# A table of ranks, and fewer planning passes, for the order of a four-stage transformer kernel

## The chip, the cores and the metric

The kernel runs on one core of a Trainium2 chip. A core has five engines that run at the same time, each with its own queue of instructions taken in order: TensorE (PE: matmuls, and PEld for its weight loads), VectorE (DVE), ScalarE (ACT), GpSimd (POOL) and SyncE (SP, which here only issues DMAs). The metric is the device time of one execution in microseconds (us); less is better.

## What is computed

The input x has 16 sequences of 256 tokens with 128 features, float32. It goes through six residual steps, of four kinds:

```python
x = x + 0.5 * _L0_ffn_ref(_layernorm(x), ...)   # experts: 8, two per token, and one shared
x = x + _L0_attn_ref(_layernorm(x), ...)        # differential attention, 16 heads, causal
x = x + 0.5 * _L0_ffn_ref(_layernorm(x), ...)   # the same experts again
x = x + 0.5 * _L1_ffn_ref(_layernorm(x), ...)   # a quantised MLP, 128-512-128
x = x + _L1_attn_ref(_layernorm(x), ...)        # linear attention, a scan over tokens
x = x + 0.5 * _L1_ffn_ref(_layernorm(x), ...)   # the quantised MLP again
```

Nothing in the change touches what is computed. What differs is in which order each engine does it.

## The kernel before

**Tiling.** The tokens are cut into 8 blocks of 512 (two sequences each), and a block stays on chip as `xs[k]` from its load to its store. The two expert steps are called "a" and "b". Each treats the blocks in groups: for "a" 0, 1, 2-3, 4-5, 6-7, for "b" 0-1, 2-3, 4-5, 6, 7. Group a0 computes all eight experts densely. All other groups route: GpSimd scatters normalised rows by indirect DMAs into slots in DRAM sorted by expert (`scatter`, L714), tiles of 128 slots are loaded and multiplied by their expert's weights (`rows`, `expert`), and GpSimd gathers the results back, adding them to `xs[k]` (`gather`, L966, eight indirect DMAs for each block and two for each 128 rows). Attention runs per sequence b: `project` and `rope` make the keys and queries, `maxima` (L1247, L1264) finds row maxima on VectorE, `weights` (L1302, L1323) takes exponentials on ScalarE, `values` and `output` finish. The scores of a step fill four banks of PSUM at once, and there is one such tile, "s". The quantised MLPs are `qa` and `qb`, the linear attention is `l` with eight steps `l k f` per block (load, product, scan L1701, product L1705, matmul).

**Order.** The program is written as some hundreds of tasks, which are Python generators. A task yields one operation at a time with the engines that can do it and a planned duration. The class `Order` keeps a planned time for each engine and each buffer, and picks what is issued next: on the engine that can start first, among the operations that can start within 0.05 us of the first, the one of lowest rank.

```python
            pick = min((c for c in cands if c[0] <= first + self.SLACK), key=lambda c: (c[1], c[0]))
```

The order picked is the order of the instructions in each engine's queue. On the chip an engine then follows its queue strictly: an instruction that waits for a semaphore holds back everything behind it. Where an operation can go to two engines (a copy to ScalarE or VectorE, a product to VectorE or GpSimd), the planned times choose.

**Ranks.** A task's rank comes from the program: 1 to 5 for the groups of "a", 4.5 and 9 down to 6 for those of "b" and the quantised and linear steps behind them, 0.5 and 0.6 for `project` and `output`, 1.5 to 2.8 for loads and the clearing of slots. The attention steps `maxima`, `weights` and `values` carry ranks of their own, between -1.0 and about -0.8, on each operation or on the task. Tasks of positive rank are shifted by kind, which is the task's name up to its first dot; there are 360 such kinds:

```python
        if rank > 0.0:

            kind = name.split(".")[0]
            self.seen.add(kind)
            rank += self.moved.get(kind, 0.0)
```

A TensorE operation of rank below 0.0 counts as urgent: when one becomes ready soon, an operation of higher rank that would delay it is put off (L213 to L222).

**Search.** `best_order` (L306) runs the whole program dry, on objects that do nothing, to get the planned end of a set of shifts. It begins with no shifts. In each further pass it gives 5 kinds new random shifts between -3 and 3, and keeps them if the planned end falls. After 60 passes the program runs once more, with the best shifts, and issues real instructions. All this happens on the host before the launch.

**The planner's durations** are formulas and constants in the operations. Those that the text below speaks of:

```python
    return k * (0.16 + n * 0.00104)                              # e_dve
    return k * (0.25 + n * 0.0029)                               # e_pool
                g = yield Op([("POOL", 1.6)], kb=1, need=need)   # one gather
        g = yield dve(1.4)                                       # the scan of linear_f
                t = end + 2.0                                    # landing of a POOL DMA
```

Other names: `attention loads` and `attention loads 2` load the attention's weights (the second ends in the product hnw, L1014, on VectorE); `stats` (L505) is bn_stats and bn_aggr, L512 and L513; `gated` (L728) makes the gated product hr of an expert, with the tanh form (L740, L749, L754 or L760) until the attention's last exponential is issued, and the Silu form (L733, L737) otherwise.

Of the kernel before, what the change touches and what calls it, by code (L numbers as in the profile page):

```python
# [270 lines left out]

PLANS, MOVES, SPREAD = 60, 5, 3.0

# [20 lines left out]
@with_exitstack  # L298
def block_kernel(ctx: ExitStack, tc: tile.TileContext, t_in: dict, out: bass.AP):
    ctx.enter_context(tc.manual_schedule())  # L300
    pools = [ctx.enter_context(tc.tile_pool(name=name, bufs=1)) for name in ("const", "small", "work")]
    pools.append(ctx.enter_context(tc.tile_pool(name="ps", bufs=1, space=PSUM)))
    program(best_order(), tc.nc, tc, *pools, t_in, out)


def best_order():  # L306


    rng = random.Random(3)
    best, moved = math.inf, {}  # L310
    for _ in range(PLANS):
        trial = dict(moved)
        if best < math.inf:
            for name in rng.sample(sorted(names), MOVES):
                trial[name] = rng.uniform(-SPREAD, SPREAD)
        order = Order(trial)
        dry = Dry()
        try:
            program(order, dry, dry, dry, dry, dry, dry, dry, dry)
        except AssertionError:  # L320
            continue
        if order.end < best:
            best, moved = order.end, trial
            names = order.seen
    return Order(moved)
# [1526 lines left out]
```

## Time and profile before

| | |
|---|---|
| median of 3 runs | 1313.22 us (1311.86 to 1316.47) |
| profiled execution | 1316.87 us |
| its span, first to last instruction | 1315.2 us |
| mean granted TensorE clock | 0.965 |
| DVE waits longest in all for | ACT thr L740, 40.8 us in 38 times |
| POOL waits longest in all for | DVE mv L513, 116.4 us in 25 times |
| PE waits longest in all for | POOL state L1705, 13.9 us in 6 times |
| 120 gathers on POOL | 194.1 us busy |
| last attention exponential | before 1000 us of the span |

A profile is of one execution. "Busy" is the time in which an engine had an instruction in hand; TensorE's ends are modelled, so a busy PE isn't PE at its peak. The granted clock is the share of full speed that TensorE was allowed. A wait names the instruction that released it last. A line such as `L409 PE MATMUL` is that of a helper, so groups are told apart by the tiles: `pgu` and `poy` are an expert's first and second product, `hr` the gated product between them, `scores` the attention scores, `qpad` their maxima, `ex` their exponentials, `pol` and `state` the linear attention, `phq`, `poq` and `yq` the quantised MLP.

### The profile page before, as it was taken

What the parts mean: (1) busy time and instruction counts of PE and PEld (TensorE: products, weight loads), DVE (VectorE), ACT (ScalarE), POOL (GpSimd) and SP (SyncE); (2) the same over time, 40 slices, a digit from 0 to 9 for tenths busy, and PEclk for the clock granted to TensorE, in tenths of its full rate; (3) what the DMA queues carried; (4) which work ended last, traced back from release to release, by engine and by line L of the source; (5) the groups of instructions that cost most, each with busy time, mean ns of one, the idle gap of its engine ahead of it and who ended that gap; (6) DMA issues with size and microseconds to landing.
All of it is one profiled execution on the core that took longest, in us unless ns stands there. A gap on an engine that the chain in (4) does not pass through costs nothing. (4 is left out here: it accounts for less than half of the span.)

```text
span 1315.2 us, 32976 instructions
## 1 busy us (share of the span) xinstructions
PE 1175.2 (89%) x12480; PEld 853.7 (65%) x12480; DVE 897.6 (68%) x2059; ACT 655.5 (50%) x1163; POOL 821.7 (62%) x972
## 2 busy tenths in 40 slices
PE   6797889999899979998987799999999869898888
PEld 3465666676576667766754577767567657675566
DVE  5465667776678655594776568768748757587993
ACT  2153456554555544645633475664564524544424
POOL 4213546738862882384458735477867788779874
PEclk9898999999999989998998799999999989998989
DMA  4675563525344335445222333314445766642331
GB/s 127 147 194 132 140 161 87 143 67 125 88 128 128 52 86 159 127 105 125 69 82 27 88 90 104 88 52 110 100 129 161 206 158 169 169 127 77 93 100 33
DMA packets 213006, 149.68 MB, mean 114 GB/s; under 512 B 18544, under 2 KB 200944, under 8 KB 212848
## 3 DMA queue, kind: packets, MB, share of 16 engines
q1 hardware_dynamic: 155376, 113.70, 31.0%
q0 software_dynamic: 21120, 15.81, 6.8%
q10 hardware_dynamic: 36352, 18.07, 4.8%
q8 instruction: 99, 1.62, 0.5%
q14 instruction: 59, 0.48, 0.1%
HBM read 117.32 MB, written 30.19 MB: 112 GB/s over the span
## 5 line engine op out<-in xcount | busy, mean ns | idle before, releaser
L409 PE MATMUL pgu<-xTg,wst 128*128 128x128 f32 x1464 | 218.5, 285 | 10.9 <-DMA wst<-in_w_dram 6.1
L409 PEld LDWEIGHTS pgu<-xTg,wst 128*128 128x128 f32 x1464 | 188.7, 195 | 37.8 <-issue 19.2
L1264 DVE TENSOR_REDUCE qpad<-scores 128x8 f32<-128x2048 f32 x64 | 146.4, 2288 | 40.2 <-PE scores L413 39.7
L1323 ACT ACTIVATE ex<-scores 128x2048 f32<-128x2048 f32 x64 | 120.2, 1878 | 85.6 <-PE scores L413 85.5
L409 PE MATMUL poy<-wst,hr 128*128 128x128 f32 x732 | 117.3, 287 | 20.2 <-POOL hr L754 9.1
L413 PE MATMUL scores<-qm,kT 32*128 32x256 f32 (+1 forms) x2048 | 114.1, 349 | 16.1 <-DVE qpad L1264 9.8
L413 PE MATMUL scores<-kT,qT 32*128 32x512 f32 (+1 forms) x1024 | 113.4, 536 | 14.0 <-ACT ex L1323 4.9
L409 PEld LDWEIGHTS poy<-wst,hr 128*128 128x128 f32 x732 | 98.5, 196 | 36.8 <-DVE hr L737 11.7
L966 POOL DMA_INDIRECT x<-slots_yb,pos x64 | 106.5, 1664 | 17.5 <-issue 15.8
L928 ACT ACTIVATE y<-poy,xg 128x128 f32<-128x128 f32 x162 | 59.2, 368 | 98.0 <-PE poy L409 93.1
L413 PEld LDWEIGHTS scores<-qm,kT 32*128 32x128 f32 x2048 | 79.6, 189 | 41.5 <-DVE qpad L1264 16.2
L413 PE MATMUL pav<-ex,vaug 128*32 128x512 f32 (+1 forms) x1024 | 98.4, 503 | 2.3 <-ACT ex L1323 2.2
L966 POOL DMA_INDIRECT x<-slots_ya,pos x56 | 87.6, 1565 | 17.2 <-issue 14.2
L500 POOL TENSOR_TENSOR rr<-ss,mhalf 128x32 f32<-128x32 f32 x16 | 87.9, 5492 | 16.5 <-DVE ss L1401 16.4
L714 POOL DMA_INDIRECT slots_xa<-xng,pos x56 | 56.0, 1001 | 61.3 <-DMA slots_xa<-xng,pos 30.4
L413 PEld LDWEIGHTS pol<-owr,state 128*128 128x128 f32 x512 | 68.5, 207 | 37.9 <-POOL state L1705 18.9
L413 PE MATMUL pol<-owr,state 128*128 128x128 f32 x512 | 74.8, 295 | 20.3 <-POOL state L1705 13.9
L516 POOL TENSOR_SCALAR rs<-mv 128x4 f32<-128x4 f32 (+1 forms) x56 | 19.8, 353 | 117.2 <-DVE mv L513 116.4
L1701 DVE TENSOR_TENSOR_SCAN state<-lam,kv 128x512 f32<-128x512 f32 x64 | 90.3, 1423 | 1.4 <-POOL kv L1698 1.1
L413 PEld LDWEIGHTS <-shift 32*128 32x128 bf16 x3072 | 59.2, 95 | 48.3 <-issue 37.5
L714 POOL DMA_INDIRECT slots_xb<-xng,pos x64 | 67.6, 1057 | 35.4 <-DMA slots_xb<-xng,pos 13.5
L1247 DVE TENSOR_REDUCE qpad<-scores 128x16 f32<-128x2048 f32 x32 | 73.2, 2289 | 22.7 <-PE scores L413 22.4
(250 smaller groups left out, 2651.8 us busy)
## 6 DMA issues: line engine op xcount, KB each, us to landing
wst<-in_w_dram SPq DMA_DIRECT2D x573, 128.0 KB
kv<-values_l SPq DMA_DIRECT2D x64, 256.0 KB
xg<-slots_xb SPq DMA_DIRECT2D x21, 258.0 KB
slots_yb<-y ACTq DMA_DIRECT2D x21, 256.0 KB
xg<-slots_xa SPq DMA_DIRECT2D x18, 258.0 KB
slots_ya<-y ACTq DMA_DIRECT2D x18, 256.0 KB
slots_xa<-zero ACTq DMA_DIRECT2D x10, 258.0 KB
slots_xb<-zero ACTq DMA_DIRECT2D x10, 258.0 KB
```

Of the source, the lines that this page charges most:

```text
L409: nc.tensor.matmul(dst, lhsT, rhs, start=start, stop=stop)
L413: nc.tensor.matmul(dst, lhsT, rhs, start=start, stop=stop, skip_group_check=True)
L500: nc.gpsimd.tensor_tensor(dst, src, mhalf[:, :n], ALU.pow)
L516: nc.gpsimd.tensor_scalar(rs, mv[:, 0:nt, 1], LN_EPS, None, ALU.add)
L714: ins = nc.gpsimd.indirect_dma_start(sx, by_rows(r["pos"][:, i * nt + t : i * nt + t + 1]), xn[:, t, :], None,)
L928: nc.scalar.activation(y[:, i, :], po[:, 0:D], AF.Copy, scale=xg[:, i, D:SW])
L966: nc.gpsimd.indirect_dma_start(x[:, t, :], None, sy, by_rows(r["pos"][:, a : a + 1]), compute_op=ALU.add,)
L1247: nc.vector.tensor_reduce(qp[:, 0, T0 : T0 + 2, :, :, HD].rearrange("p t m g -> p m t g"), s.rearrange("p m (t g n) -> p m t g n", t=2, g= ...
L1264: nc.vector.tensor_reduce(qp[:, 1, T, :, :, HD], s.rearrange("p m (g n) -> p m g n", g=G), AX.X, ALU.max, negate=True)
L1323: nc.scalar.activation(ex0, s, AF.Exp, scale=1.0 / math.sqrt(HD))
L1701: nc.vector.tensor_tensor_scan(state, lam, kv, 0.0, ALU.mult, ALU.add)
```

## The change

The search no longer begins with no shifts but with a table of them, `MOVED`, that stands in the source. It has shifts for 228 of the 360 kinds, each with one decimal, between -3.0 and 2.9. The first pass plans with the table as it is; the other 19 change 5 kinds each, as before, with the same seed. The planner, the durations and the program are otherwise the same.

```diff
-PLANS, MOVES, SPREAD = 60, 5, 3.0
+MOVED = {
+    "attention consts": 2.6, "attention loads": 2.0, "attention loads 2": -1.0, "attention pads": 0.8,
...
+    "experts a2": 2.1, "experts a3": -0.1, "experts a4": 0.1, "experts b1": -0.8, "experts b2": -2.5,
+    "gather a1": -1.0, "gather a2": -1.0, "gather a3": 2.2, "gather a4": 1.7, "gather b0": 1.6,
+    "gather b4": 0.6, "l 0": 0.4, "l 0 0": 0.2, "l 0 1": -0.8, "l 0 2": 1.3, "l 0 3": 0.7, "l 0 4": 0.5,
...
+    "output 1": 1.2, "output 11": 2.5, "output 14": -0.1, "output 2": 1.6, "output 3": 1.9, "output 5": 2.9,
+    "output 6": 0.5, "output 8": -2.3, "output 9": 0.2, "project 0": -2.5, "project 10": -1.8,
+    "project 11": -1.9, "project 14": 2.2, "project 15": -1.9, "project 2": -0.4, "project 5": -0.8,
+    "project 7": -0.9, "project 9": -1.3, "qa 0 0": -0.6, "qa 0 1": 2.7, "qa 0 2": -2.0, "qa 1": -1.0,
...
+    "route b4": 1.8, "rows a4": 0.6, "scatter a1": 1.3, "scatter a2": 2.3, "scatter a3": -0.0,
+    "scatter a4": 2.7, "scatter b0": -1.7, "scatter b1": -1.3, "scatter b2": -0.3, "scatter b3": -0.4,
...
+    "softmax b4": 1.8, "x1": -1.3, "x2": 0.7, "x5": 0.9, "x6": -1.7, "x7": 1.0,
+}
+
+
+PLANS, MOVES, SPREAD = 20, 5, 3.0
...
     rng = random.Random(3)
-    best, moved = math.inf, {}
+    best, moved = math.inf, dict(MOVED)
     for _ in range(PLANS):
         trial = dict(moved)
         if best < math.inf:
```

## The prediction

> **What bounds the kernel now.** I read the busy shares first, then the slices, three stages, and in each stage the largest holes of TensorE with what ended them.
>
> ```profile
> PE 1175.2 (89%) x12480; PEld 853.7 (65%) x12480; DVE 897.6 (68%) x2059; ACT 655.5 (50%) x1163; POOL 821.7 (62%) x972
> PE   6797889999899979998987799999999869898888
> POOL 4213546738862882384458735477867788779874
> PEclk9898999999999989998998799999999989998989
> ```
>
> TensorE is the bound: 1175.2 of 1315.2 us. After the start the PE digit falls to 7 or 6 in slices 15, 22, 23 and 33; POOL stands at 7 or 8 in each, and the granted clock falls to 8 or 7. The stages:
>
> ```profile
> 0.00:150.00 150.00, 118.05 (x755) 82.40 (x755) 85.21 (x322) 52.24 (x100) 49.71 (x125) 0.94 0.61 152
> 150.00:990.00 840.00, 774.82 (x9984) 552.86 (x9977) 570.28 (x1257) 458.21 (x761) 520.02 (x601) 0.97 0.39 101
> 990.00:1315.20 325.20, 282.32 (x1756) 218.43 (x1748) 242.12 (x480) 145.04 (x304) 251.98 (x247) 0.95 0.47 129
> ```
>
> The second column is the stretch, then busy PE, PEld, DVE, ACT and POOL, then clock, DMA share, GB/s. PE idles 32.0 us in the dense start, 65.2 under attention, 42.9 in the tail: 140.0 us, the most that any reordering could win at unchanged PE work. The largest hole under attention:
>
> ```profile
> 717.88 2.09 PE L413 MATMUL scores<-kT,qT 32*128 32x512 f32 x8
> ...
> 722.98 2.09 PE L413 MATMUL scores<-kT,qT 32*128 32x256 f32 x16
> ...
> 727.89 2.09 PE L413 MATMUL scores<-qm,kT 32*128 32x256 f32 x16 [2.39 <-DVE qpad L1247]
> ...
> 732.22 2.09 PE L413 MATMUL scores<-kT,qT 32*128 32x512 f32 x8 [2.03 <-ACT ex L1323]
> ```
>
> Only attention is left to issue there: one scores tile, filled, reduced, filled again. The filler (experts, quantised layers, linear attention) hangs on sixteen gathers:
>
> ```profile
> 722.57 1.55 POOL L966 DMA_INDIRECT x<-slots_yb,pos  x1 [0.30 <-issue]
> 724.42 1.56 POOL L966 DMA_INDIRECT x<-slots_yb,pos  x1 [0.30 <-issue]
> 726.28 1.55 POOL L966 DMA_INDIRECT x<-slots_yb,pos  x1 [0.30 <-issue]
> ```
>
> The tail's largest hole is of another kind:
>
> ```profile
> 1053.63 0.29 DVE L512 BATCH_NORM_STATS2 st<-x 128x6 f32<-128x128 f32 x1 [4.62 <-DMA x<-slots_yb,pos]
> ...
> 1055.18 0.39 DVE L737 SCALAR_TENSOR_TENSOR hr<-thr,pgu 128x256 f32<-128x256 f32 x1
> ```
> ```profile
> 1055.62 1.23 PE L409 MATMUL poy<-wst,hr 128*128 128x128 f32 x4 [6.06 <-DVE hr L737]
> ```
>
> VectorE's queue held a statistics instruction whose gathered rows had not landed; the expert's product stood behind it, and PE waited 6.06 us for that product.
>
> **Nothing is added on the device but order.** The planner runs before launch, so the table and the drop from 60 passes to 20 cost no device time. Each task still issues its operations and DMAs; which engine takes an elementwise operation, and which form the gated product has, follow the new plan. PE work therefore stays at 1175 us, moved by its clock alone. The kernel before ends its search with 29 of 360 kinds moved. The table moves 228 and leaves 132; if each accepted pass places 5 of 360 at random, (1 - 5/360)^n = 132/360 gives n = 72 accepted passes, against 6 before. It is a much longer climb on the planner's own clock, so what counts is how far that clock agrees with the chip.
>
> **Where the planner is right, it can gain.** It knows coarse things: that attention without filler starves PE, that a block's work waits for its gathers. Three holes have the size for it.
> - 706 to 740 us: the seven gaps of PE are 1.05+1.49+2.82+1.98+2.39+2.03+0.71 = 12.5 us. The matmuls between run slowly too: a scores block takes 2.09 us where the same block took 1.14 at 713.14 us (four blocks, 3.8 us), the value product 2.79 against 1.50 (1.3), the masks 0.4 more. That is 12.5 + 5.5 = 18.0 us. The Trainium skill, "TensorE: Matmul & The Clock Gate" (Part 1), ties the half clock to an idle window of about 3.4 us; by the rule no gap here (longest 2.82) would cost more than itself, so 12.5. The trace has clock 0.50 at 720 to 730 us with PE busy 5.63 of 10, so I take the row: 18.0.
> - 1048 to 1100 us: PE is busy 36.79 of 52 at clock 0.87: 15.2 idle and 36.79 x 0.13 = 4.8 slow, 20.0 us.
> - 50 to 70 us: VectorE waits 11.59 us for the load of the head norm (L1014), with the product of the shared expert behind it; PE idles 9.0 us and is busy 10.99 at 0.74, 2.9 slow: 11.9 us. "attention loads" goes up 2.0 and "attention loads 2" down 1.0, so the load and this instruction both move. It may vanish or come back elsewhere: no sign can be read.
>
> Together 49.9 us. The ranks reach them: gathers of a3, a4 and b0 and the scatters and experts around them get shifts of 1 to 3, and project 0, 10, 11 and 15 fall below -1.0, ahead of all attention steps. What ranks can't reach are the attention steps (each operation carries its own rank), the first 12.4 us without PE (the first loads are not moved) and the arithmetic. SP's queue changes order with them, and that costs nothing: its weight loads wait 436.5 us in all for buffers that the expert products free, and PE waits only 6.1 us for weights; without that cover each late load would cost PE up to the 2.5 us that is the longest now. A gap filled here takes filler from elsewhere, and there is no row for a hole that stays closed: the bounds are 0 and 49.9, and I take half, 25, because two of the three are of kinds that the planner sees.
>
> **Where the planner is wrong, the order costs.** A gather is planned at 1.6 us of POOL, and the trace starts one every 1.86 us (722.57, 724.42, 726.28). Sixteen in a row end 16 x 0.26 = 4.2 us later than planned. What is queued next on POOL, or on VectorE behind a wait for the landing, is late by that much, and PE stands on it:
>
> ```profile
> PE poy L409 <- POOL hr L754: 9.1, 3, 4.2
> PE poy L409 <- DVE hr L737: 8.0, 3, 6.1
> ```
>
> Three bursts do this now: 4.23 us at 464, 4.2 at 590, 6.06 at 1050: 14.5 us, 4.8 each, of nine bursts (120 gathers, 7.5 of 16). A climb removes idle time which the planner sees and knows nothing of this slack. I take five bursts in place of three: 2 x 4.8 = 9.7 us back. Bounds: none stalls (-14.5) to all nine (+29).
>
> The same goes for VectorE beside POOL. The Trainium skill, "SBUF — State Buffer" (SBUF: two separate sides), says that a VectorE operation with two SBUF inputs and a GpSimd one that reads SBUF take a shared port pair in turn, the later one blocked for the whole of the other; the planner lets them overlap. Row: the 64 scans (L1701) take 1216 ns in the median, 1423 in the mean, so 64 x 0.207 = 13.2 us are lost now. If every scan met a POOL product (median 1316 ns) from its start, the rule would give 64 x 1.316 = 84 us. POOL and VectorE are both over 74% busy in the tail already and mostly don't collide; by the row a new order moves the 13.2 us by a few either way, and I take 0.
>
> **Sum.** -25 + 9.7 = -15 us. The profiled execution took 1316.87 us, 1.7 around its span of 1315.2; it should read about 1301. The median of the runs shown is 1313.22, 3.7 below the profiled execution; from it the forecast is 1313.2 - 15 = 1298 us.
>
> **Rivals.**
> - *The plan is tighter than the chip (slower).* Place: POOL's queue after each gather burst, and VectorE's queue behind statistics that wait for landings. Price 4.8 us a burst. If all nine bursts stall, +29, and the seen gain is only the smallest hole's size, 8 to 12, the sum is +19: 1332 us. It decides once the stalls added, times 4.8, exceed the seen gain: over five bursts at 25 us, over two at 10. For it: PE's slack is only 11%, the three stalls are in a plan that was climbed six steps, and 72 steps select for tightness. Against: six of nine bursts are harmless now, and POOL's products are planned too dear (1.735 us for 512 columns, 1.316 measured), which gives slack back.
> - *The gain lies where the chip has none (no change).* In the tail the planner charges a scan 1.4 us (1.216 in the trace) and a VectorE product of 512 columns 0.88 (0.68): for 64 scans and 65 products, 11.8 + 13 = 25 us too much. A climb that unloads VectorE there wins time which the chip never spent. The seen gain falls to about 10, the new stalls take 9.7: 1313 us.
> - *The change doesn't do what it says.* If its one-decimal ranks aren't those of the plan found, the first pass starts from a disturbed plan and nineteen trials of five moves (six of 59 were accepted before) recover little: 1305 to 1330. All 228 names exist among the kinds, so it isn't idle. I count its chance into the first two.
>
> **Chances.** Forecast 0.50; tighter than the chip 0.38; no change 0.12. A difference under 0.3%, about 4 us, can't be told from none here. The forecast's own range is 1278 to 1309: holes all but closed with stalls unchanged, down to a quarter closed. The slower case runs from 1318 to 1345. Leaving out a tenth at either end gives 1277 to 1336. Faster 0.49, same 0.13, slower 0.38.
>
> **What would show it.** Right: PE idle falls from 140 to about 125 us with PE busy at 1165 to 1178; no stretch of 30 us with POOL gathering and PE under 70%; the hole near 1050 shorter. Stalls: the waits of the expert's second product on POOL or VectorE products, 17 us together now, grow to about 27; at over 45 the first rival holds. Wrong for another reason: more PE busy time (clock below 0.96), VectorE's scan mean above 1.5 us, or new waits of attention on its own projections, which the moved project ranks could bring and which I priced at nothing since none of the longest waits of PE is of that kind.

## The result, and the profile after

| | before | after |
|---|---|---|
| median, 20 runs each | 1311.98 us (1309.07 to 1316.74) | 1319.13 us (1312.27 to 1327.89) |
| ratio, 95% interval | | 1.0051 [1.0037, 1.0065] |
| profiled execution | 1316.87 us, slower than any of these runs | 1312.27 us, the fastest of its runs |
| its span | 1315.2 us | 1310.5 us |
| TensorE idle, by the stages' sums | 140.0 us | 145.7 us |

The changed kernel is 0.5% slower: 7.2 us, where 15 us less were forecast. The two profiles stand in the opposite order to the medians, since that of before is of a longer execution than its median and that of after of its shortest. They can show where time was lost and won, but the difference of their spans is not the result.

The busy shares and slices of the kernel after:

```profile
PE 1164.8 (89%) x12480; PEld 847.5 (65%) x12480; DVE 896.8 (68%) x2047; ACT 653.5 (50%) x1167; POOL 828.5 (63%) x974
PE   6787869999998999998998799998899988998887
POOL 4213544667655686457464856489783688789883
PEclk9899979999999999999999899999999999998999
```

The weak slices 15, 22 and 33 of before stand at 8 or 9 now. A new one has come at slice 6 (a PE digit of 6, a clock of 7), and slice 23 still reads 7. The stages, with the columns as before:

```profile
0.00:150.00 150.00, 118.07 (x763) 81.99 (x764) 84.35 (x322) 53.34 (x101) 52.03 (x126) 0.95 0.62 154
150.00:990.00 840.00, 766.24 (x9901) 553.52 (x9903) 585.41 (x1259) 448.11 (x754) 536.82 (x612) 0.98 0.39 102
990.00:1310.50 320.50, 280.53 (x1822) 212.01 (x1814) 227.06 (x467) 152.07 (x313) 239.65 (x236) 0.99 0.47 128
```

The idle time under attention rose from 65.2 to 73.8 us. The last attention exponential starts at 998.06 us (987.21 before), so 10.9 us were lost up to there, and the rest after it is 15.6 us shorter (312.4 for 328.0). Now slice 6, on ScalarE:

```profile
158.79 0.38 ACT L970 ACTIVATE y<-poy,xg 128x128 f32<-128x128 f32 x1
166.44 0.37 ACTq L978 DMA_DIRECT2D slots_ya<-y  x1
166.85 1.88 ACT L1365 ACTIVATE ex<-scores 128x2048 f32<-128x2048 f32 x1 [7.68 <-DMA wst<-in_w_dram]
```

The store of y (group a1) had its data at 159.2 us and was issued at 166.44. ScalarE's queue stood 7.3 us at it, with an attention exponential behind, and what ended the wait is named in the bracket: a load of expert weights. (The Trainium skill, "DMA: Bandwidth & Descriptors", says in "Anatomy of one DMA — SWDGE (gpsimd) path", of the DMA engines in general, that a wait for a semaphore is made by the sequencer that issues the DMA, before the transfer is handed on; the trace agrees for this store on ScalarE's queue, since the exponential behind it starts only once the store has been issued.) That load is on SP's queue, which had stood itself:

```profile
150.80 0.38 SPq L469 DMA_DIRECT2D wst<-in_w_dram  x1
162.68 0.38 SPq L910 DMA_DIRECT2D xg<-slots_xa  x1
163.64 0.34 SPq L467 DMA_DIRECT2D wst<-in_w_dram  x1
```

```profile
SPq L910 <- DMA slots_xa<-xng,pos: 11.4, 1, 11.4
```

The first fence is SP's timeline, the second its waits: SP waited 11.4 us for the scatter of group a2 before it could load a2's first rows, and the weights went out behind that. On TensorE and GpSimd this came of it:

```profile
168.78 2.09 PE L455 MATMUL scores<-kT,qT 32*128 32x512 f32 x8 [5.00 <-ACT ex L1365]
...
189.31 1.22 PE L451 MATMUL poy<-wst,hr 128*128 128x128 f32 x4 [4.98 <-POOL hr L796]
```
```profile
171.20 1.62 POOL L1008 DMA_INDIRECT x<-slots_ya,pos  x1 [9.78 <-DMA xg<-slots_xa]
```

TensorE waits 5.00 us for the held exponential, then runs a scores block in 2.09 us in place of 1.14. The gathers need the stored rows; GpSimd idles 9.78 us and begins them at 171.20 us. The burst of eight runs to 185.8, a gated product stands behind it, and TensorE waits 4.98 us for that.

**Why a store waits for a load on another queue.** The built program has it. Each DMA of SP's and ScalarE's queues signals its end on one of eight semaphores. The layer that records the program deals these out round-robin over both queues in one order of its own, and makes a DMA wait for the one that had the semaphore before, the eighth before it. Where that order isn't the plan's, a store can wait for a load that the plan issues later. Before, no store does so; after, two do: the last store of group a1 (for weights behind a2's rows) and that of b0 (for b1's rows). The second shows at 710.93 us:

```profile
704.40 0.37 ACT L970 ACTIVATE y<-poy,xg 128x128 f32<-128x128 f32 x1
710.93 0.37 ACTq L978 DMA_DIRECT2D slots_yb<-y  x1
711.34 0.40 ACT L443 COPY oall<-pto 128x288 f32<-128x288 f32 x1 [6.57 <-DMA xg<-slots_xb]
```

It is held 6.2 us. GpSimd idles 9.52 us before the sixteen gathers that need these rows, and begins them at 715.94. On VectorE and TensorE:

```profile
729.33 0.29 DVE L554 BATCH_NORM_STATS2 st<-x 128x6 f32<-128x128 f32 x1 [5.77 <-DMA x<-slots_yb,pos]
```
```profile
735.01 2.09 PE L455 MATMUL scores<-qm,kT 32*128 32x256 f32 x16 [6.04 <-DVE qpad L1289]
```

VectorE stood 5.77 us at statistics whose rows had not landed, the maxima of attention stood behind, and TensorE waited 6.04 us for them. It is again a slow block of 2.09 us.

### The profile page after: what moved, and what is told of

The parts are those of the page before. It is cut to its first block, busy times and chain, and to the rows that moved or that the text cites. A ratio compares the mean times of both kernels' runs of the same rounds, so it can differ in the third digit from the quotient of the medians.

```text
span 1310.5 us, 32942 instructions
## 1 busy us (share of the span) xinstructions
PE 1164.8 (89%) x12480; PEld 847.5 (65%) x12480; DVE 896.8 (68%) x2047; ACT 653.5 (50%) x1167; POOL 828.5 (63%) x974
## 5 line engine op out<-in xcount | busy, mean ns | idle before, releaser
L451 PE MATMUL pgu<-xTg,wst 128*128 128x128 f32 x1464 | 217.9, 284 | 13.6 <-DMA wst<-in_w_dram 6.6
L1365 ACT ACTIVATE ex<-scores 128x2048 f32<-128x2048 f32 x64 | 120.1, 1877 | 73.1 <-PE scores L455 65.2
L455 PE MATMUL scores<-qm,kT 32*128 32x256 f32 (+1 forms) x2048 | 114.4, 350 | 20.8 <-DVE qpad L1306 13.3
L791 DVE SCALAR_TENSOR_TENSOR hr<-thr,pgu 128x256 f32<-128x256 f32 x132 | 54.3, 415 | 57.5 <-ACT thr L782 56.2
L1743 DVE TENSOR_TENSOR_SCAN state<-lam,kv 128x512 f32<-128x512 f32 x64 | 89.2, 1407 | 3.6 <-POOL kv L1740 3.4
L455 PE MATMUL pol<-owr,state 128*128 128x128 f32 x512 | 70.6, 283 | 17.3 <-POOL state L1747 10.4
```

Source lines behind the costliest of these rows:

```text
L451: nc.tensor.matmul(dst, lhsT, rhs, start=start, stop=stop)
L455: nc.tensor.matmul(dst, lhsT, rhs, start=start, stop=stop, skip_group_check=True)
L791: nc.vector.scalar_tensor_tensor(h, th, 1.0, pg, ALU.add, ALU.mult)
L1365: nc.scalar.activation(ex0, s, AF.Exp, scale=1.0 / math.sqrt(HD))
L1743: nc.vector.tensor_tensor_scan(state, lam, kv, 0.0, ALU.mult, ALU.add)
```

## The experiments

A first theory was A: the two held stores are the loss, and without them the plan's gain arrives. Its rival B: the plan is too tight for the chip, above all because gathers are priced at 1.6 us and come every 1.86. The planned ends, on the planner's own clock, are 1348.0 us with no shifts, 1314.3 for the kernel before and 1289.1 for the table; the twenty passes accept no move, so the kernel after runs the table as it stands. All ratios below are to the kernel before.

**1. Both stores freed.** The kernel after, with the first load of each group's rows made to wait for the y store recorded last. This changes the recording order, so the stores no longer wait for these loads; the order of instructions on each of the five queues is the same as in the kernel after.

```diff
+    stores = []
...
-        nc.sync.dma_start(xg[:, 0:n, :], sx[:, 4 * q : 4 * q + n, :])
+        ins = nc.sync.dma_start(xg[:, 0:n, :], sx[:, 4 * q : 4 * q + n, :])
+        if q == 0 and stores and not isinstance(ins, Dry):
+            tc.add_manual_dep(
+                ins.ins, stores[-1].ins.name,
+                mybir.DependencyInfo(mybir.DependencyClass.Sync, mybir.DependencyReason.DATA), reason="behind the store",
+            )
...
-            nc.scalar.dma_start(sy[:, s - i : s + 1, :], y[:, 0 : i + 1, :])
+            stores.append(nc.scalar.dma_start(sy[:, s - i : s + 1, :], y[:, 0 : i + 1, :]))
```

> The changed kernel with the same order in all five queues. Added: the first load of gathered rows of each group on SP waits for the store of expert results that stands before it in the plan, so that no store on ScalarE takes a DMA semaphore whose previous user is a load that SP issues later. Theory A (stores held back by a shared semaphore): ScalarE no longer idles 7.3 us before the store at 166 us and 6.2 us before the one at 711 us, the holes of PE behind them (5.0 and 3.0 us, and part of 5.0 at 184 and 6.0 at 729) shrink, and the time falls by 8 to 15 us, to 1304 to 1311. Theory B (gathers planned at 1.6 us and started every 1.86): nothing changes but those two waits, within 3 us of 1319.

1296.30 us (1295.18 to 1298.43), ratio 0.9896 [0.9875, 0.9918]. The same three lines of ScalarE's timeline in this run:

```profile
155.32 0.38 ACT L977 ACTIVATE y<-poy,xg 128x128 f32<-128x128 f32 x1
155.74 0.37 ACTq L985 DMA_DIRECT2D slots_ya<-y  x1
160.56 1.88 ACT L1372 ACTIVATE ex<-scores 128x2048 f32<-128x2048 f32 x1 [4.85 <-PE scores L455]
```

The store goes out 0.04 us after its data and the exponential waits for its scores alone. TensorE and GpSimd behind it:

```profile
162.49 1.14 PE L455 MATMUL scores<-kT,qT 32*128 32x512 f32 x8 [2.01 <-ACT ex L1372]
...
177.22 0.71 PE L451 MATMUL poy<-wst,hr 128*128 128x128 f32 x4 [1.02 <-POOL hr L796]
```
```profile
159.10 1.62 POOL L1015 DMA_INDIRECT x<-slots_ya,pos  x1 [0.19 <-issue]
```

Counted from the start of the y before the store (158.79 us with the store held, 155.32 freed), the scores block comes at 10.0 us held and 7.2 freed, the first gather at 12.4 and 3.8, the second product at 30.5 and 21.9. So most of ScalarE's 7.68 us was not lost, since the exponential would have waited for its scores anyway: by that way TensorE is 2.8 us late, and 8.6 us behind the late gathers.

With the same order of instructions the kernel goes from 0.5% slower to 1.0% faster; the gain was more than A had expected.

**2 and 3. One store at a time.** The condition `q == 0` becomes `(w, j, q) == ("a", 2, 0)`, which frees the store of a1, or `("b", 1, 0)`, which frees that of b0.

> The changed kernel with the first of the two stores freed alone (group a1, at 166 us in its trace); the one at 711 us stays held. Theory A: about half of what freeing both brought (from 1319 to 1296 us), so 1305 to 1311. If the early one matters more because all later work inherits its delay: below 1303.

> The changed kernel with the second store freed alone (group b0, at 711 us). Theory A: the other half, 1305 to 1311; if the early one carries nearly all, 1315 or more.

With a1's store freed 1304.56 us, ratio 0.9956 [0.9938, 0.9973]; with b0's freed 1309.07 us, 0.9990 [0.9978, 1.0001]. In each the other store is still held, by 6.1 and 7.2 us. From 1.0051, the first store is worth 0.95% (12.5 us) and the second 0.61% (8.0 us). Together that is 1.56%, and both freed gave 1.55%: within the intervals the two add up, and nothing of the loss is left over. Each costs more than its hold (7.3 and 6.2 us). For the first, 8.6 us stand behind the late gathers (run 1); where the rest arises isn't shown.

**4. The edit in the kernel before,** where no store is held: a control.

> The kernel before with the edit of e1_own_order, which in it frees no store, because none is held. Theory A: the same as before within 3 us. If the edit itself makes kernels faster (loads that no longer crowd, fewer waits elsewhere): 5 us or more below before.

0.9994 [0.9982, 1.0006]: the edit as such is worth nothing.

**5. The hold put into the kernel before.** In the kernel before, the last store of a1 waits for the first rows of a2 to land.

```diff
+    stores = {}
...
-        nc.sync.dma_start(xg[:, 0:n, :], sx[:, 4 * q : 4 * q + n, :])
+        ins = nc.sync.dma_start(xg[:, 0:n, :], sx[:, 4 * q : 4 * q + n, :])
+        if (w, j, q) == ("a", 2, 0) and (w, j - 1) in stores and not isinstance(ins, Dry):
+            tc.add_manual_dep(
+                stores[w, j - 1].ins, ins.ins.name,
+                mybir.DependencyInfo(mybir.DependencyClass.Sync, mybir.DependencyReason.DATA), reason="behind the rows",
+            )
...
-            nc.scalar.dma_start(sy[:, s - i : s + 1, :], y[:, 0 : i + 1, :])
+            stores[w, j] = nc.scalar.dma_start(sy[:, s - i : s + 1, :], y[:, 0 : i + 1, :])
```

> The kernel before, unchanged in all queues, with one wait added: the last store of group a1 on ScalarE (at 160 us) waits until the first rows of group a2 are loaded (issued at 163 us, landed near 166), which is what the shared semaphore did in the changed kernel. Theory A: the exponentials behind it are late by some 6 us and the time goes up by 4 to 12 us, to 1314 to 1322. If the changed kernel's loss belongs to its order and not to the wait: within 3 us of before.

1319.01 us, ratio 1.0075 [1.0056, 1.0094]. ScalarE idles 5.6 us before that store, GpSimd 8.64 us before the gathers behind it (2.15 in the profile of before), and the kernel loses 9.8 us. Such a hold costs this much in another order too.

**6. How much of a planned gain the chip gives.** The kernel before without its search (`PLANS` 60 to 1), a plan that is 34 us longer.

> The kernel before with one planning pass, so that no rank is moved; its plan ends 34 us later than that of before and 59 us later than that of the changed kernel, on the planner's own clock. If the planner's gains reach the chip in full, it takes 1346 us; if half of them do, 1329. If the chip follows the plan only coarsely and tight plans stall (theory B), it lies near before: 1312 to 1325.

1330.57 us, ratio 1.0155 [1.0128, 1.0183]: 20.8 us for 34 planned, 0.6 of them. In run 1 it was 13.6 (0.0104 of 1311.98) for 25.1, 0.54. The planner's clock is worth something, at a bit over half.

**7. The gather at its measured pitch.** The price of a gather is set to 1.86 us, and the table is climbed further under it (6520 passes, 28 accepted); the stores are freed as in run 1.

```diff
-                g = yield Op([("POOL", 1.6)], kb=1, need=need)
+                g = yield Op([("POOL", 1.86)], kb=1, need=need)
...
-PLANS, MOVES, SPREAD = 20, 5, 3.0
+PLANS, MOVES, SPREAD = 1, 5, 3.0
```

> The planner with a gather at 1.86 us of POOL instead of 1.6, ranks climbed anew from the table under that price (one pass here), and the edit of e1_own_order, so no store is held. Theory B (bursts of gathers that end 4.2 us late cost PE 4 to 6 us each): the stalls of the second expert product on POOL's product go, and it is 7 us or more below e1_own_order (ratio 0.9896), at 0.984 or less. If the pitch hardly matters: another plan of the same quality, ratio 0.986 to 0.994.

1279.64 us (1276.27 to 1286.14), ratio 0.9781 [0.9755, 0.9807], faster than both kernels. Its busy shares and slices:

```profile
PE 1153.8 (90%) x12480; PEld 840.5 (66%) x12480; DVE 899.6 (70%) x2052; ACT 659.5 (52%) x1177; POOL 818.9 (64%) x957
PE   6787889999999999978999999998999979898997
PEclk9899999999999999999999999999999999999999
```

Against the profile of run 1 (span 1294.5, TensorE busy 1161.8), the span of 1276.1 us is 18.4 shorter, 10.4 by idle time and 8.0 by TensorE's busy time, for the same number of matmuls (mean granted clock 0.986 for 0.981). GpSimd's timeline shows what the price did to a burst of gathers:

```profile
713.73 1.55 POOL L1021 DMA_INDIRECT x<-slots_yb,pos  x1 [0.30 <-issue]
716.27 0.22 POOL L564 TENSOR_SCALAR rs<-mv 128x2 f32<-128x2 f32 x1 [0.99 <-DVE mv L561]
716.58 0.73 POOL L548 TENSOR_TENSOR rs<-rs,mhalf 128x2 f32<-128x2 f32 x1
717.50 1.94 POOL L1021 DMA_INDIRECT x<-slots_yb,pos  x1 [0.20 <-issue]
```

The sixteen no longer come in one row: other work of GpSimd goes between them.

**8. The other measured prices too.** As run 7, with GpSimd's and VectorE's products, the scan (1.25 us) and the issue of DMAs at what the traces show, and a climb under those (6428 passes, 42 accepted).

> As e7_gather_price, with these prices also set near the trace: POOL products (0.17 + 0.0022 per column), VectorE products from SBUF (0.16 + 0.00108), the scan 1.25, and DMA issues 0.48 us on SP and 0.42 on ScalarE each instead of 0.07. If the planner's prices limit what a climb brings: ratio below 0.985. If they don't: 0.986 to 0.994.

1289.29 us, ratio 0.9848 [0.9825, 0.9872]: just inside what was expected, and worse than run 7. More prices set right did not give more here. One climb each can't say whether the prices or the chance of the climb made that difference.

**9 to 11. Price or climb?** Run 7 differs from run 1 by a price and by a longer climb. Three controls, all with the freed stores: a climb from no shifts at the old price (4378 passes), the table climbed further at the old price (6459 passes), and a climb from no shifts at 1.86 us (4423 passes). Their code is that of run 7 with another table, and with 1.6 in the first two.

> The old prices, but ranks from another climb, begun with no shifts and another seed, whose plan ends at 1296.6 on the planner's clock (before 1314.3, the table 1289.1), with the edit of e1_own_order. If a planned gain reaches the chip by 0.54 of its size, as it did in e1_own_order (13.5 of 25.1): 1309.5 - 0.54 x 17.7 = 1300, ratio 0.993. If the table was a lucky plan: ratio 1.0 within 0.003.

> The table climbed for 6459 more passes at the old price of a gather, 1.6 us (10 accepted, planned end 1286.2 for the table's 1289.1), with the two stores freed. The control to the run with the price of 1.86 us, which had the same start, length of climb and freed stores. Reckoned with gathers at 1.86 us, this plan ends at 1334.7, the table at 1334.3, the kernel before at 1353.2. If the price made the gain of that run (theory): no better than the table with freed stores, 0.986 to 0.993 of the time before. If a longer climb as such made it (rival): below 0.983.

> A climb from no shifts with the gather priced at 1.86 us (4423 passes, 31 accepted, planned end 1300.6 on that clock, 1339.6 on the old one), with the two stores freed. The control to the other climb, which began with no shifts too and had nearly as many passes at the old price (planned end 1296.6, but 1342.2 when gathers are reckoned at 1.86). If the price decides (theory): 0.976 to 0.986 of the time before, as for the table climbed further at that price. If what the table holds decides and a climb from nothing can't reach it (rival): 0.995 or more.

They gave 1.0021 [1.0006, 1.0035], 0.9879 [0.9858, 0.9900] and 0.9892 [0.9872, 0.9912]. Run 9 came out where its rival put it, with the table as a lucky plan. Run 10 has run 7's start and length of climb and only the old price, and it is no better than the table. Run 11 lies between what the theory and the rival expected of it, so it confirms neither in full, but it is 1.3% below run 9, its control. All plans with freed stores, by their planned end on either clock:

| plan | gather at 1.6 us | gather at 1.86 us | measured ratio |
|---|---|---|---|
| before (run 4) | 1314.3 | 1353.2 | 0.9994 |
| climb from none, 1.6 (run 9) | 1296.6 | 1342.2 | 1.0021 |
| table, climbed further, 1.6 (run 10) | 1286.2 | 1334.7 | 0.9879 |
| table (run 1) | 1289.1 | 1334.3 | 0.9896 |
| table, climbed further, 1.86 (run 7) | 1315.6 | 1301.4 | 0.9781 |
| climb from none, 1.86 (run 11) | 1339.6 | 1300.6 | 0.9892 |

On the old clock the fastest kernel is planned slower than the kernel before. The new clock puts it among the best two, but it doesn't order all: run 9 is planned 11 us better than before and is not, and run 11 is 1.1% above run 7 at the same planned end. From run 10 to 7 the time falls by 0.98%, from 9 to 11 by 1.3%, of which up to 0.8% may be a loss that run 9 owes to the edit or to its chip (run 12). With the new price TensorE waits less for gated products, first in run 10, then in run 7:

```profile
PE poy L454 <- POOL hr L799: 5.5, 2, 2.9
PE poy L454 <- DVE hr L782: 5.1, 6, 1.5
```
```profile
PE poy L457 <- POOL hr L802: 2.7, 2, 2.3
PE poy L457 <- DVE hr L785: 1.1, 2, 0.9
```

That is 10.6 us against 3.8, about half of what was gained; from run 9 to 11 it is 15.3 against 9.5. So the price probably brings about 1%. It isn't shown beyond doubt: each plan is one climb, and two plans of the same price and nearly the same planned end, runs 7 and 11, are 1.1% apart.

**12. Run 9 without the edit.** In run 9 SP stood 14.8 us for the landing of a store, by the wait that the edit adds, and TensorE then waited for weights.

> The other climb without the edit that frees the stores. In its run with the edit, SP stood 14.8 us at the first rows of group a2 for the landing of the store of a1, and TensorE waited 2.7 and 5.9 us for expert weights behind it at 116 and 133 us, at a clock of 0.76 to 0.90. Without the edit one store of a1 can be held by the rows of a2 in its place. If the edit's own wait is what that climb lost (theory): 0.990 to 0.998 of the time before, and no wait for weights over 3 us between 110 and 140 us. If the plan itself holds no gain on the chip (rival, as its end of 1342.2 with gathers at 1.86 us says): 1.000 or more.

Ratio 0.9941 [0.9916, 0.9966], on a chip where the kernel before took 1347.57 us. The ratio is the one expected, but the reason isn't shown:

```profile
137.89 1.20 PE L433 MATMUL pgu<-xTg,wst 128*128 128x128 f32 x4 [6.12 <-DMA wst<-in_w_dram]
```

TensorE waits for the same weights, 4.31 and 6.12 us, so the edit had not made that wait. The two ratios of this plan, 0.9941 and 1.0021, are 0.8% apart; whether by the edit or by the other chip stays open.

## Why the prediction was wrong

**The step that failed** is the one that let SP's queue change order: "and that costs nothing". It asked only whether weights would be late for TensorE, and they were not (6.6 us of waits, 6.1 before). What SP's new order held was ScalarE's queue, through the semaphores that both queues share. That had no term: 12.5 + 8.0 = 20.5 us by runs 2 and 3. Without it the ratio is 0.9896, which is 1298 us for a before of 1312, and 1298 was forecast; with it, 1319. The trace of before showed the stores of y in ScalarE's queue, with exponentials and copies behind them; what a store waits for, and who stands behind it, was not asked.

**The holes, -25.** With the stores freed the sum is -13.6 us for the -15 of the forecast. That the two agree is in part luck. The other term, +9.7, came out at -5 (below), the wait of 6.06 us at 1055 us stood in both terms, and the gain lies in one place. The last attention exponential in run 4, the kernel before with the edit, and in run 1:

```profile
980.05 1.88 ACT L1330 ACTIVATE ex<-scores 128x2048 f32<-128x2048 f32 x1 [1.26 <-PE scores L413]
```
```profile
982.22 1.88 ACT L1372 ACTIVATE ex<-scores 128x2048 f32<-128x2048 f32 x1 [0.93 <-PE scores L455]
```

From there to the end of the span run 4 takes 328.4 us (to 1308.5) and run 1 takes 312.3 (to 1294.5). The tail is 16.1 us shorter, which is all of the gain; up to there none is seen, so what was filled in the two earlier holes came back elsewhere, as the prediction had said it might. (In the longer profile of before the tail takes 328.0 us too, but the exponential comes at 987.21, so a few us up to there can't be told.) By holes, in the kernel after as it is:

```profile
50.00:70.00 20.00, 11.48 (x45) 7.36 (x44) 5.41 (x18) 3.47 (x6) 4.49 (x9) 0.74 0.60 129
706.00:740.00 34.00, 24.91 (x306) 19.53 (x302) 14.63 (x25) 10.74 (x17) 20.58 (x15) 0.85 0.51 113
1048.00:1100.00 52.00, 42.42 (x288) 33.60 (x286) 35.87 (x87) 21.29 (x48) 44.77 (x48) 1.00 0.79 198
```

At 1048 to 1100 us TensorE is busy 42.42 of 52 at full clock, where it was 36.79 at 0.87: of 20.0 us that it cost, 9.6 are left. At 706 to 740 us it is 24.91 for 21.53, and what is left is the second held store; in run 1, where these gathers lie at 690 to 724 us, it is 29.78. At 50 to 70 us nothing changed (VectorE still waits 11.29 us for the head norm); no sign had been read there.

**Two more bursts stalling, +9.7.** This term was mis-sized, with the wrong sign. The waits of the expert's second product on gated products were 17 us and should have grown to 27:

```profile
PE poy L451 <- POOL hr L796: 12.2, 5, 5.0
...
PE poy L451 <- DVE hr L779: 4.4, 6, 1.1
```

They are 16.6 us in the kernel after, of which 4.98 is the burst that the held store delayed; with the stores freed they are 7.2 + 4.7 = 11.9, so 5 us less than before. So the first rival, which put the loss into GpSimd's queue after gathers, is not what made this kernel slower. But its ground holds: the gather's price was wrong, and setting it right probably brought about 1% (runs 7 to 11).

**The second rival**, a gain that the chip doesn't have, would have given 1313 us, 6 us from the measured time, but not for its reason: run 1 shows that the gain is there. That the change does what it says is shown by the planned ends: the table's own plan is what runs.

**The clock** was priced within each hole, which was right in kind, but its share was larger. From run 4 to run 1 the span falls by 14.0 us: 7.6 are TensorE's busy time (1169.4 to 1161.8, for 12480 matmuls each, at a mean granted clock of 0.965 and 0.981) and 6.4 its idle time. The prediction had TensorE's busy time fall to 1165 at most. VectorE's scans beside GpSimd, which it took at 0, stayed as they were: 1407 ns in the mean in the kernel after, for 1423.

## What to carry to other kernels

When an order changes, ask of every queue what its DMAs wait for, not only what waits for them: a short store that stands at the head of a compute engine's queue can hold that engine for a load on another queue. Before a longer search on a model, set the prices in the model that the trace contradicts, above all of what comes in bursts; here that went with the fastest kernel. A planned gain reached the chip at 0.54 and 0.6 in two cases, and in another not at all or at 0.44 (runs 9 and 12), so it is a guess until it is run.

## What was not expected of the hardware

DMAs on ScalarE's queue stood 7.3 and 6.2 us for DMAs on SP's, though the profile lists the two queues apart, through completion semaphores that they share by the way the program is recorded. A hold of 5.6 to 7.3 us on ScalarE cost the kernel 8 to 12.5 us. The runs of the kernel after spread over 15.6 us, those of run 1, with the same order on each queue, over 3.3. These are 20 runs and 5, so the number of runs is part of that; the rest isn't explained.
